# W1's products with the norm's factors ahead of the first ten adjacency chunks, and the edges' check behind them

## The chip, the cores and the metric

The kernel runs on one core of one Trainium2 chip. The metric is the time of one execution on the device, in microseconds. Three executions of the kernel before took 1035.32, 1038.75 and 1046.16 us; the median is 1038.75 us. A further execution was recorded by the hardware profiler: it took 1032.22 us, with a span of 1030.4 us between its first and last instruction. All rows of the trace quoted here are of that execution.

The engines have short names throughout: PE is the matrix engine (PEld its weight loads), DVE the vector engine, ACT the scalar engine, POOL the general engine and SP the one that issues most transfers. Each works through its own instructions in the order of the program and waits at an instruction until the semaphores that it names have come. L353 is line 353 of the kernel.

## What is computed

The layer takes 1250 tokens x of width 768 and 21250 edges (20000 drawn ones, and a loop for each token), sorted by destination. It adds to x a two-layer graph attention network and a kernelised attention, both on the normalised x, and then a mixture of 8 experts.

```python
xn = _layernorm(x)
x_norm = layer_norm(xn, norm_g, norm_b)              # the norm's factors: norm_g and norm_b
out1 = gat_conv(x_norm, src, dst, W1, a_src1, a_dst1, b1, 4, 192, N)
out2 = gat_conv(out1, src, dst, W2, a_src2, a_dst2, b2, 2, 96, N)
gnn = concatenate([x, out2], -1) @ Wu + bu
x = x + gnn + mix(xn)                                # kernelised attention, 12 heads
x = x + ffn(_layernorm(x))                           # 8 experts, 2 per token
# gat_conv: h = x @ W; e = leaky_relu(s_src[src] + s_dst[dst]) with s = (h * a).sum(-1)
#           alpha = softmax of e over the edges of one dst; out = sum alpha * h[src] + bias
```

Two parts of this matter for the change. The first is the adjacency: the kernel turns the list of edges into a dense matrix of counts, 1250 by 1250, so that the attention over edges becomes matrix products with a mask. The second is the product of W1 with the norm's factors: since x_norm is a scaled and shifted row, its product with W1 needs norm_g and norm_b multiplied into W1.

## The kernel before

The tokens are cut into ten tiles of 125. The edges are cut into 170 chunks of 125 in order of destination. A chunk holds edges of one destination tile, or of two where it lies near a border; this is true of edges that are spread evenly enough, and a check of the edges' tiles (L261 to L270) tells whether it is true of the edges given. Its result goes into the last column of the tile `bad`, which is read much later, to choose between this path and a general one.

`adjacency()` (L289) builds the counts. For each chunk c, DVE makes two one-hot tiles: `ohs` (L342) for the source, packed into 313 columns, and `ohd` (L346) for the destination. PE multiplies them into the sum `pe` of the destination tile (L353). There are five `ohs` tiles and four `ohd` tiles, used in turn, so DVE can be no more than four chunks ahead of PE. When a tile's last chunk is in, ACT copies the sum out and DVE takes the packed counts apart (L296 to L308). `adjacency()` is a generator: `adj(n)` (L366) runs n chunks, and the program calls it between other work.

The first stage of the program does the following. SP fetches the edges, W1 in three parts of 768 KB (L187) and x; ACT fetches the small arrays and W2. DVE and PE turn the edge lists so that a chunk lies along the partitions (L247 to L250), and DVE makes the packed source columns (L253 to L259). DVE then runs the check, and ten chunks follow (L371). Next DVE makes the columns of R, the products of W2 with its score vectors: four products and four sums (L394, L398). PE meanwhile multiplies W1 with norm_g and norm_b (L403): 12 products of a 128 by 2 weight, each of which the trace shows as two records. ACT copies the result into v1 (L408), and PE turns v1 by 8 small transposes, `by_channels` (L411).

Then comes a loop over the four heads. In each, PE transposes W1's two halves (L434), ACT copies them into wT (L435), PE multiplies wT with R (pw, L444) and ACT stores the result, scaled by norm_g, as W12 (L447). After each half and after every third product `beside(h)` (L419) runs two more chunks of the adjacency, and in the last heads also pieces of x's normalisation. At the end of a head, PE makes the constant columns from vv, the result of `by_channels` (pc, L453).

PE and DVE run this whole part in the order in which the program is written: it stands inside a manual schedule (L233 to L468). So DVE takes the check, ten chunks, R and the following chunks in just this order, and PE ten chunks, L403, the transposes and so on. Some tiles share buffers: `off` of the check, `pr` of R, `v1` and `wT` all use three buffers under the tag wT, one after the other in the order of the program.

After this stage come the transposes of x and the rest of the adjacency, beside the keys of the kernelised attention; the two attention layers; the update and the routing; and the experts.

Of the kernel before, what the change touches and what calls it, by code (L numbers as in the profile page):

```python
# [9 lines left out]
F32 = mybir.dt.float32  # L10
# [4 lines left out]
ALU = mybir.AluOpType  # L15
AX = mybir.AxisListType
# [3 lines left out]
D = 768  # L20
P = 125
NT = N // P
KD = D // 128
# [17 lines left out]
NCH = NEDGE // P  # L41
# [5 lines left out]
SLACK = 2  # L47
# [26 lines left out]
def kernel(  # L74
# [3 lines left out]
    nc = tc.nc  # L78
    ctx.enter_context(nc.allow_non_contiguous_dma("small vectors, laid out by partition"))

    def opened(**kw):
        p = tc.tile_pool(**kw)
        return p, p.__enter__()
# [42 lines left out]
    def stats_of(pool, src_tile, mv_col, tag):  # L126
        st = pool.tile([P, 2, 6], F32, tag="bnst", name=f"st_{tag}")
        for i in range(2):
            nc.vector.bn_stats(out=st[:, i, :], in_=src_tile[:, i * 384 : (i + 1) * 384])
        nc.vector.bn_aggr(out=mv_col, in_=st)  # L130

    def rstd_of(pool, mv, tag, t0, t1):

        ve = pool.tile([P, t1 - t0], F32, tag="lnve", name=f"ve_{tag}_{t0}")
        nc.vector.tensor_scalar(ve, mv[:, t0:t1, 1], 1e-5, None, op0=ALU.add)
        sd = pool.tile([P, t1 - t0], F32, tag="lnsd", name=f"sd_{tag}_{t0}")
        nc.scalar.activation(sd, ve, AF.Sqrt)
        rs = pool.tile([P, t1 - t0], F32, tag="lnrs", name=f"rs_{tag}_{t0}")
        nc.vector.reciprocal(rs, sd)
        return rs  # L140
# [36 lines left out]
    ps_, ps = opened(name="ps", bufs=2, space=PSUM)  # L177
# [5 lines left out]
    def weight(pool, ap, name, eng):  # L183
        w = pool.tile([128, KD, D], F32, tag="mw", name=name)
        r = ap.rearrange("(k p) n -> p k n", p=128)
        for k in range(0, KD, 2):
            eng.dma_start(out=w[:, k : k + 2, :], in_=r[:, k : k + 2, :])  # L187
        return w


    wgc_, wgc = opened(name="wgc", bufs=1)
    wg_, wg = opened(name="wg", bufs=2)
    gb = wgc.tile([128, KD, 2], F32, name="gb")
# [8 lines left out]
    w1_sb = weight(wgc, W1, "w1_sb", nc.sync)  # L202
# [32 lines left out]
    edges = {}  # L235
    iota = edc.tile([P, N], I16, name="iota")
    nc.gpsimd.iota(iota, pattern=[[1, N]], base=0, channel_multiplier=0)
    bad = edc.tile([P, NT + 1], F32, name="bad")
# [12 lines left out]
    for i in range(1, NPK):  # L251
# [5 lines left out]
            nc.vector.tensor_scalar(wgt, up, step, 1.0, op0=ALU.mult, op1=ALU.add)  # L257
        else:
            nc.vector.scalar_tensor_tensor(wgt, up, step, wgt, op0=ALU.mult, op1=ALU.add)  # L259

    mid_t = wgc.tile([P, NT, 17], F32, name="mid")  # L261
    nc.gpsimd.iota(mid_t, pattern=[[P, NT], [0, 17]], base=0, channel_multiplier=0, allow_small_or_imprecise_dtypes=True)
    mid = mid_t.rearrange("p a b -> p (a b)")
    off = wg.tile([P, 2, NCH], F32, tag="wT", name="off", bufs=3)
    nc.gpsimd.memset(off, 0.0)
    nc.vector.tensor_tensor(off[:, 0, SLACK:], edges["dst"][:, SLACK:], mid[:, : NCH - SLACK], ALU.is_lt)
    hi = wgc.tile([P, NCH], F32, tag="up1", name="hi", bufs=1)
    nc.vector.tensor_scalar(hi, edges["dst"], float(P), None, op0=ALU.subtract)
    nc.vector.tensor_tensor(off[:, 1, : NCH - SLACK], hi[:, : NCH - SLACK], mid[:, SLACK:], ALU.is_ge)
    nc.vector.tensor_reduce(bad[:, NT : NT + 1], off.rearrange("p a c -> p (a c)"), AX.X, ALU.max)  # L270

    def with_loops(rows, t):

        own = rows[:, t * P : (t + 1) * P]
        nc.vector.tensor_tensor(own, own, identb, ALU.add)
# [90 lines left out]
    def adj(n=NCH):  # L366
        for _ in range(n):
            if next(steps, 0) == 0:
                break

    adj(10)  # L371

    def normalised(g):

        t0, t1 = g * GT, (g + 1) * GT
        for t in range(t0, t1):
            stats_of(ln, acc[:, t, :D], mv1[:, t, :], f"a{t}")
            yield
        rs1 = rstd_of(ln, mv1, "a", t0, t1)
        yield  # L380
        for t in range(t0, t1):
            xn = acc[:, t, :D]
            nc.vector.tensor_scalar(
                xn, xn, mv1[:, t, 0:1], rs1[:, t - t0 : t - t0 + 1], op0=ALU.subtract, op1=ALU.mult
            )
            yield
# [4 lines left out]
    for h in range(H2):  # L391
        for i in range(2):
# [3 lines left out]
                a2[:, i, h * C2 : (h + 1) * C2].unsqueeze(1).to_broadcast([CH, 2 * H1, C2]), ALU.mult,  # L396
            )
            nc.vector.tensor_reduce(R[:, :, score_col[h][i] : score_col[h][i] + 1], pr, AX.X, ALU.add)  # L398

    pv1 = [ps.tile([2, D // 2], F32, tag="ac", name=f"pv1_{i}") for i in range(2)]  # L400
    for k in range(KD):
        for i in range(2):
            nc.tensor.matmul(  # L403
                pv1[i], gb[:, k, :], w1_sb[:, k, i * (D // 2) : (i + 1) * (D // 2)], start=(k == 0), stop=(k == KD - 1)
            )
    v1 = wg.tile([2, D], F32, tag="wT", name="v1", bufs=3)
    for i in range(2):
        nc.scalar.copy(v1[:, i * (D // 2) : (i + 1) * (D // 2)], pv1[i])  # L408
    vv = wgc.tile([CH, 2 * H1, 2], F32, name="vv")

    def by_channels():  # L411
        pv2 = ps.tile([CH, 2 * H1, 2], F32, tag="ac", name="pv2")
        for q in range(2 * H1):
            nc.tensor.transpose(pv2[:, q, :], v1[:, q * CH : (q + 1) * CH], ident[:2, :2])
        nc.scalar.copy(vv, pv2)

    early = (piece for g in range(2) for piece in normalised(g))

    def beside(h):  # L419

        for _ in range(2):
            adj(1)
            if h >= 2:
                next(early, 0)

    for h in range(H1):
        wT = []
        for j in range(2):
            wT.append(wg.tile([CH, D], F32, tag="wT", name=f"wT_{h}_{j}", bufs=3))
            q0 = (2 * h + j) * CH  # L430
            for b0, n in ((0, 4), (4, 2)):
                pt = ps.tile([128, 4, 128], F32, tag="tr", name=f"w1t_{h}_{j}_{b0}")
                for i in range(n):
                    nc.tensor.transpose(pt[:CH, i, :], w1_sb[:, b0 + i, q0 : q0 + CH], ident)  # L434
                nc.scalar.copy(  # L435
                    wT[j][:, b0 * 128 : (b0 + n) * 128].rearrange("p (a c) -> p a c", c=128), pt[:CH, :n, :]
                )
            beside(h)
        if h == 0:
            by_channels()  # L440
        for k in range(KD):
            pw = ps.tile([128, GW], F32, tag="pk", name=f"pw_{h}_{k}")
            for j in range(2):
                nc.tensor.matmul(  # L444
                    pw, wT[j][:, k * 128 : (k + 1) * 128], R[:, 2 * h + j, :], start=(j == 0), stop=(j == 1)
                )
            nc.scalar.activation(W12[:, k, h * GW : (h + 1) * GW], pw, AF.Copy, scale=gb[:, k, 0:1])  # L447
            if k in (2, 5):
                beside(h)
        for i, cb in enumerate((c1b, c0b)):  # L450
            pc = ps.tile([P, GW], F32, tag="ac", name=f"pc_{h}_{i}")
            for j in range(2):
                nc.tensor.matmul(  # L453
                    pc, vv[:, 2 * h + j, i : i + 1].to_broadcast([CH, P]), R[:, 2 * h + j, :],
                    start=(j == 0), stop=(j == 1),
                )
            nc.scalar.copy(cb[:, h * GW : (h + 1) * GW], pc)
# [86 lines left out]
    with tc.tile_pool(name="kpp", bufs=1) as kpp:  # L544
# [55 lines left out]
        for t0, n in ((0, 4), (4, 4), (8, 2)):  # L600
            pst = ps.tile([2 * H1, 4 * P], F32, tag="tr", name=f"pst_{t0}")
            for k in range(KD):
                nc.tensor.matmul(
                    pst[:, : n * P], wsc[:, k].rearrange("p h i -> p (h i)"), xnT[:, k, t0 * P : (t0 + n) * P],
                    start=(k == 0), stop=(k == KD - 1),
# [164 lines left out]
    with tc.If(flag > 0):  # L770


        with tc.tile_pool(name="gd", bufs=1) as gd, tc.tile_pool(name="ps_g", bufs=1, space=PSUM) as ps_g:
            for own, other in (("dst", "src"), ("src", "dst")):
# [6 lines left out]
                for tiles in PASSES:  # L781
# [3 lines left out]
                    c = 0  # L785
# [885 lines left out]
```

## Time and profile before

| | |
|---|---|
| median of three executions | 1038.75 us (1035.32 to 1046.16) |
| profiled execution | 1032.22 us, span 1030.4 us |
| ten chunks on PE | 11.62 to 15.99 us |
| L403 on PE, 24 records | 15.99 to 24.84 us |
| check of the edges on DVE, 4 instructions | 9.74 to 11.05 us |
| R on DVE, 8 instructions | 15.40 to 22.80 us |
| HBM read, written | 74.77 MB, 27.04 MB |

A row of a timeline gives the start in us from the beginning of the span, the duration in us, the engine, the line, the operation, the tile written and the tiles read, the sizes, and how many instructions were merged; in brackets stands how long the engine had been idle and what ended that. Consecutive instructions of one kind are merged, so the ten chunks are one row of PE. The granted clock is the share of full speed at which the matrix engine was allowed to run. Its record begins at 18.07 us, and for the time before that the tables print 1.00.

### The profile page before, as it was taken

Reading aid. Unit: us, or ns where it says so; the run is one execution under the profiler, and the core shown is the slowest. Engines: PE = TensorE matmul, PEld = TensorE weight load, DVE = VectorE, ACT = ScalarE, POOL = GpSimd, SP = SyncE. Lnnn points to the kernel's source line nnn. Section 1 sums busy time; section 2 is a strip of 40 time slices with the busy share of each in tenths; the row PEclk is TensorE's granted clock in tenths of the full one; section 3 lists DMA queues with packets and bytes.
Section 4 is the critical chain, followed back from the end, with each engine's and each line's share of the span. In section 5 each row is a group of like instructions: output and inputs, shape, how many; then the busy total and the mean of one; then the engine's idle time right before and its main releaser. Section 6 shows DMA issues by size and latency. Waiting matters only on the chain. (4 is left out here: it accounts for less than half of the span.)

```text
span 1030.4 us, 12127 instructions
## 1 busy us (share of the span) xinstructions
PE 955.1 (93%) x4323; PEld 655.1 (64%) x4323; DVE 635.3 (62%) x1407; ACT 386.2 (37%) x662; POOL 137.1 (13%) x148
## 2 busy tenths in 40 slices
PE   6899999999999999999999999999998889999970
PEld 2785455545665476777776865567678667767750
DVE  7699555304858467677768839255687554445441
ACT  0653333310000075555655800064566254323320
POOL 1001010000000000000000012110100311357633
PEclk9999999999999999999999999999998889999995
DMA  8410000032241100000023323111252357356443
GB/s 205 146 50 18 19 15 23 25 124 106 80 149 60 51 34 1 25 25 25 2 79 119 113 73 115 51 56 45 86 184 97 123 183 248 100 185 176 154 126 90
DMA packets 55169, 92.43 MB, mean 90 GB/s; under 512 B 22697, under 2 KB 29033, under 8 KB 55099
## 3 DMA queue, kind: packets, MB, share of 16 engines
q1 hardware_dynamic: 30970, 73.64, 20.7%
q0 software_dynamic: 15904, 17.02, 5.9%
q10 hardware_dynamic: 8224, 0.89, 0.7%
q8 instruction: 39, 0.64, 0.3%
q14 instruction: 32, 0.25, 0.1%
HBM read 74.77 MB, written 27.04 MB: 99 GB/s over the span
## 5 line engine op out<-in xcount | busy, mean ns | idle before, releaser
L852 PEld LDWEIGHTS pa_a<-acc,p_a 125*125 125x125 f32 x800 | 133.6, 187 | 17.1 <-issue 6.7
L852 PE MATMUL pa_a<-acc,p_a 125*125 125x197 f32 x800 | 141.6, 332 | 0.8 <-DVE h L876 0.5
L842 ACT ACTIVATE e_a<-rowt_a,s 125x625 f32<-125x625 f32 x80 | 64.8, 816 | 127.4 <-DMA rowt_a<-ab_d 93.1
L715 PE MATMUL pg<-W,xnT 128*125 128x396 f32 x240 | 81.7, 498 | 1.8 <-DVE acc L718 1.8
L922 PE MATMUL po<-wu_sb,xnT 128*125 128x384 f32 x240 | 81.7, 488 | 1.3 <-issue 1.3
L530 PE MATMUL pk_q<-xnT,wq_sb 128*128 128x375 f32 (+1 forms) x216 | 81.6, 516 | 0.7 <-DVE acc L718 0.7
L530 PE MATMUL pk_k<-xnT,wk_sb 128*128 128x375 f32 (+1 forms) x216 | 82.0, 515 | 0.0
L848 DVE SCALAR_TENSOR_TENSOR p_a<-e_a,cntT 125x625 f32<-125x625 f32 x80 | 64.0, 806 | 28.7 <-PE pa_a L852 26.9
L846 DVE SCALAR_TENSOR_TENSOR e_a<-e_a,e_a 125x625 f32<-125x625 f32 x80 | 64.2, 807 | 22.9 <-ACT e_a L842 15.8
L493 DVE CUSTOM_DVE_ANT_0 junk<-nmr,rows 125x1250 f32<-125x1250 bf16 x40 | 58.4, 1459 | 29.2 <-DMA nmr<-nm_d 16.0
L346 DVE TENSOR_SCALAR ohd<-iota,dst_f 125x125 bf16<-125x125 int16 (+1 forms) x170 | 51.4, 302 | 39.9 <-PE pe L353 39.9
L1520 PE MATMUL po<-ew,hT 128*125 (+1 forms) x192 | 67.1, 493 | 5.5 <-DVE hT L1311 5.0
L844 ACT ACTIVATE e_a<-rowt_a,s1x 125x625 f32<-125x625 f32 x80 | 64.3, 815 | 18.7 <-DVE e_a L846 18.1
L1291 PE MATMUL ph<-ew,xTe 128*125 (+1 forms) x288 | 68.9, 390 | 0.0
L715 PEld LDWEIGHTS pg<-W,xnT 128*125 128x125 f32 x240 | 44.5, 188 | 34.8 <-DVE acc L718 2.4
L922 PEld LDWEIGHTS po<-wu_sb,xnT 128*125 128x125 f32 x240 | 44.4, 189 | 31.0 <-issue 2.0
L1291 PEld LDWEIGHTS ph<-ew,xTe 128*125 128x125 f32 x288 | 55.4, 195 | 11.8
L530 PEld LDWEIGHTS pk_q<-xnT,wq_sb 128*128 128x128 f32 x216 | 39.8, 189 | 33.5 <-issue 14.3
L342 DVE TENSOR_SCALAR ohs<-iota,smod,wgt 125x313 bf16<-125x313 int16 x170 | 60.5, 356 | 0.0
L852 PE MATMUL pa_b<-h,p_b 125*125 125x97 f32 x400 | 53.4, 285 | 6.7 <-issue 2.3
L852 PEld LDWEIGHTS pa_b<-h,p_b 125*125 125x125 f32 x400 | 51.3, 201 | 11.2 <-issue 4.7
L530 PEld LDWEIGHTS pk_k<-xnT,wk_sb 128*128 128x128 f32 x216 | 38.5, 189 | 23.3 <-issue 9.7
(348 smaller groups left out, 1459.0 us busy)
## 6 DMA issues: line engine op xcount, KB each, us to landing
y_d<-y SPq DMA_DIRECT2D x23, 375.0 KB
ew<-in_w1T SPq DMA_DIRECT2D x8, 768.0 KB
ew<-in_w2T SPq DMA_DIRECT2D x8, 768.0 KB
nmr<-nm_d SPq DMA_DIRECT2D x20, 305.2 KB
rowt_a<-ab_d SPq DMA_DIRECT2D x8, 610.4 KB
x_d<-acc SPq DMA_DIRECT2D x10, 376.0 KB
acc<-in_x SPq DMA_DIRECT2D x10, 375.0 KB
xr<-in_x SPq DMA_DIRECT2D x10, 375.0 KB
```

Of the source, the lines that this page charges most:

```text
L342: nc.vector.tensor_scalar(oh_s[:, :TH], iota[:, :TH], smod[:, c : c + 1], wgt[:, c : c + 1], op0=ALU.is_equal, op1=ALU.mult)
L493: nc.vector.tensor_tensor_reduce(out=junk, in0=nm, in1=row, scale=1.0, scalar=-3.0e38, op0=ALU.add, op1=ALU.max, accum_out=mx_col)
L530: nc.tensor.matmul(pk[:, :w], w_sb[:, k, f * 128 : (f + 1) * 128], xnT[:, k, t0 * P : (t0 + n) * P], start=(k == 0), stop=(k == KD - 1),)
L715: nc.tensor.matmul(pg, xnT[:, k, t * P : (t + 1) * P], W12[:, k, cs], start=(k == 0), stop=(k == KD - 1))
L842: nc.scalar.activation(e1, rowt[:, 0, :], AF.Exp, bias=s[:, h, 0, u : u + 1])
L844: nc.scalar.activation(e2, rowt[:, 1, :], AF.Exp, bias=sx[:, h, u : u + 1])
L846: nc.vector.scalar_tensor_tensor(e1, e1, 1.0, e2, op0=ALU.min, op1=ALU.max)
L848: nc.vector.scalar_tensor_tensor(p, e1, 1.0, cntT[:, u, hf * HN : (hf + 1) * HN], op0=ALU.min, op1=ALU.mult)
L852: nc.tensor.matmul(pas[i][:, :cw], p[:, i * P : (i + 1) * P], hv, start=(u == 0), stop=(u == NT - 1))
L922: nc.tensor.matmul(po[:, hf, :384], xnT[:, k, ts], wu_sb[:, k, cs], start=(k == 0), stop=False)
L1291: nc.tensor.matmul(ph, xT[:, k, :], ew1[:, whose_r[q], k, :].rearrange("p o i -> p (o i)"), start=(k == 0), stop=(k == KD - 1),)
L1520: nc.tensor.matmul(po[:, hf, :384], hT[:, c, :], ew2[:, e_r, c, hf * 384 : (hf + 1) * 384].rearrange("p o n -> p (o n)"), start=(c == 0), ...
```

## The change

Three pieces of the program change places, and nothing is added or taken away. W1's products (L403) and the two copies into v1 (L408) stand ahead of the call of the first ten chunks. The check of the edges stands behind these ten chunks, with POOL's iota and memset for it. `by_channels` stands directly ahead of the loop over the heads, no longer inside its first turn.

```diff
-    mid_t = wgc.tile([P, NT, 17], F32, name="mid")
-    nc.gpsimd.iota(mid_t, pattern=[[P, NT], [0, 17]], base=0, channel_multiplier=0, allow_small_or_imprecise_dtypes=True)
-    mid = mid_t.rearrange("p a b -> p (a b)")
-    off = wg.tile([P, 2, NCH], F32, tag="wT", name="off", bufs=3)
-    nc.gpsimd.memset(off, 0.0)
-    nc.vector.tensor_tensor(off[:, 0, SLACK:], edges["dst"][:, SLACK:], mid[:, : NCH - SLACK], ALU.is_lt)
-    hi = wgc.tile([P, NCH], F32, tag="up1", name="hi", bufs=1)
-    nc.vector.tensor_scalar(hi, edges["dst"], float(P), None, op0=ALU.subtract)
-    nc.vector.tensor_tensor(off[:, 1, : NCH - SLACK], hi[:, : NCH - SLACK], mid[:, SLACK:], ALU.is_ge)
-    nc.vector.tensor_reduce(bad[:, NT : NT + 1], off.rearrange("p a c -> p (a c)"), AX.X, ALU.max)
...
+    pv1 = [ps.tile([2, D // 2], F32, tag="ac", name=f"pv1_{i}") for i in range(2)]
+    for k in range(KD):
+        for i in range(2):
+            nc.tensor.matmul(
+                pv1[i], gb[:, k, :], w1_sb[:, k, i * (D // 2) : (i + 1) * (D // 2)], start=(k == 0), stop=(k == KD - 1)
+            )
+    v1 = wg.tile([2, D], F32, tag="wT", name="v1", bufs=3)
+    for i in range(2):
+        nc.scalar.copy(v1[:, i * (D // 2) : (i + 1) * (D // 2)], pv1[i])
     adj(10)
+    mid_t = wgc.tile([P, NT, 17], F32, name="mid")
...
+    nc.vector.tensor_reduce(bad[:, NT : NT + 1], off.rearrange("p a c -> p (a c)"), AX.X, ALU.max)
...
+    by_channels()
     early = (piece for g in range(2) for piece in normalised(g))
...
-        if h == 0:
-            by_channels()
```

In the changed kernel W1's products are line L363, the copies into v1 L368, the first chunks' product L341, the check L373 to L381, R L404 and L408, and pw L443.

More of the change, by code (lines that the diff above doesn't have):

```diff
@@ L369, in adj @@
                 break
-    adj(10)
+    pv1 = [ps.tile([2, D // 2], F32, tag="ac", name=f"pv1_{i}") for i in range(2)]
[7 more added lines that the diff above has]
+        nc.scalar.copy(v1[:, i * (D // 2) : (i + 1) * (D // 2)], pv1[i])
+    adj(10)
+    mid_t = wgc.tile([P, NT, 17], F32, name="mid")
+    nc.gpsimd.iota(mid_t, pattern=[[P, NT], [0, 17]], base=0, channel_multiplier=0, allow_small_or_imprecise_dtypes=True)
+    mid = mid_t.rearrange("p a b -> p (a b)")
+    off = wg.tile([P, 2, NCH], F32, tag="wT", name="off", bufs=3)
+    nc.gpsimd.memset(off, 0.0)
+    nc.vector.tensor_tensor(off[:, 0, SLACK:], edges["dst"][:, SLACK:], mid[:, : NCH - SLACK], ALU.is_lt)
+    hi = wgc.tile([P, NCH], F32, tag="up1", name="hi", bufs=1)
+    nc.vector.tensor_scalar(hi, edges["dst"], float(P), None, op0=ALU.subtract)
+    nc.vector.tensor_tensor(off[:, 1, : NCH - SLACK], hi[:, : NCH - SLACK], mid[:, SLACK:], ALU.is_ge)
+    nc.vector.tensor_reduce(bad[:, NT : NT + 1], off.rearrange("p a c -> p (a c)"), AX.X, ALU.max)
     def normalised(g):
@@ L398 @@
             nc.vector.tensor_reduce(R[:, :, score_col[h][i] : score_col[h][i] + 1], pr, AX.X, ALU.add)
[L400 to L408, printed above, removed]
     vv = wgc.tile([CH, 2 * H1, 2], F32, name="vv")
```

## The prediction

> **What bounds the kernel now.** I read the page's busy shares first. TensorE is busy over nine tenths of the span, and its row of slices stands at 9 from the third slice to the thirtieth, so a delay that reaches TensorE early has hardly anywhere to be absorbed. The change lies in the first 35 us, where the shares say nothing, so I read next a table of stretches (columns: busy us and count of PE, PEld, DVE, ACT, POOL; granted clock; DMA share; GB/s).
>
> ```profile
> PE 955.1 (93%) x4323; PEld 655.1 (64%) x4323; DVE 635.3 (62%) x1407; ACT 386.2 (37%) x662; POOL 137.1 (13%) x148
> ...
> 16.00:24.80 8.80, 8.80 (x25) 2.07 (x24) 8.66 (x17) 1.75 (x2) 0.00 (x0) 1.00 0.71 186
> 24.80:36.00 11.20, 10.42 (x72) 9.17 (x71) 3.05 (x14) 6.50 (x17) 0.00 (x0) 1.00 0.69 185
> 36.00:50.00 14.00, 11.86 (x79) 10.36 (x79) 12.41 (x44) 9.02 (x21) 1.29 (x1) 1.00 0.32 126
> 50.00:100.00 50.00, 46.90 (x258) 33.66 (x258) 49.92 (x184) 23.65 (x59) 4.81 (x9) 1.00 0.11 36
> ```
>
> From 16 to 24.8 both engines are full: PE makes W1's products with the factors while DVE makes the R columns. From 24.8 to 36 PE sets the pace and DVE idles for 8.1 us, held up by the ring of one-hot tiles. From 50 to 100 DVE is full. After 100 PE is (49.91 of 50 us to 150, 513 of 520 to 670). The timeline of PE and of DVE shows the order inside this:
>
> ```profile
> 11.62 4.43 PE L353 MATMUL pe<-ohs,ohd 125*125 125x314 bf16 x10 [4.66 <-DVE ohd L346]
> 15.99 8.91 PE L403 MATMUL pv<-w_sb,gb 128*2 128x384 f32 x24
> 24.84 0.86 PE L434 MATMUL w1t<-ident,w_sb 128*96 128x128 f32 x6
> 25.53 0.43 PE L353 MATMUL pe<-ohs,ohd 125*125 125x314 bf16 x2
> ...
> 27.72 2.39 PE L444 MATMUL pw<-R,wT 96*128 96x198 f32 x12
> ```
>
> ```profile
> 9.74 0.33 DVE L266 TENSOR_TENSOR off<-dst_f,mid 125x168 f32<-125x168 f32 x1
> ...
> 11.05 0.36 DVE L342 TENSOR_SCALAR ohs<-iota,smod,wgt 125x313 bf16<-125x313 int16 x1
> ...
> 15.40 0.95 DVE L394 TENSOR_TENSOR pr<-R,a 96x768 f32<-96x768 f32 x1
> ...
> 22.80 0.35 DVE L342 TENSOR_SCALAR ohs<-iota,smod,wgt 125x313 bf16<-125x313 int16 x1
> ...
> 30.29 0.29 DVE L346 TENSOR_SCALAR ohd<-iota,dst_f 125x250 bf16<-125x250 int16 x1 [2.03 <-PE pe L353]
> 35.36 0.16 DVE L296 TENSOR_SCALAR bad<-pe 125x1 f32<-125x1 f32 x1 [4.78 <-PE pe L353]
> ```
>
> The reader is to see three things. PE idles 4.66 us before the first chunk. The ten chunks then run as fast as DVE hands out pairs of one-hots (11.05 to 15.40 is 4.35 us, 0.435 a pair). And DVE's R block, 15.40 to 22.80 (7.40 us), runs wholly under PE's L403: the two 8 us blocks cover each other.
>
> Last, when does W1 arrive? L403 needs it, so this decides how early the moved products can start. SP and ACT issues that wait for a W1 part show it:
>
> ```profile
> SPq L217 <- DMA w_sb<-in_W: 8.1, 1, 8.1
> ```
>
> This is the first tile of x, issued at 13.23 when W1's second part had landed; ACT's b1T at 9.57 follows the first part in the same way and wb's second half at 15.97 the third. The trace's landings read 9.55, 13.22 and 15.83.
>
> **The change, part by part.**
>
> *Products ahead of the chunks.* PE no longer idles to 11.62; it waits for W1's first part and starts L363 (L403 of before) at 9.6. Behind this wait stand all ten chunks, which need only DVE. The 24 records of the 12 products are of two speeds in before: the first starts lie 0.640 us apart, those after 18.07 lie 0.322 apart. The first eight records (first part of W1) at the slow pitch end at 9.6 + 5.12 = 14.7. If the clock comes up there, sixteen at 0.322 make 5.15, and the products end at E = 19.9; parts two and three have landed by the time they are needed.
>
> When does the clock come up? The row first: L403 became dense at 15.99 and got fast at 18.07, 2.1 us later, but 6.4 us after the first chunk at 11.62. [...]
>
> *Chunks behind the products.* DVE starts its one-hots 1.31 us earlier (9.74, where the check stood), but it owns four ohd and five ohs tiles and stops before the fifth ohd until PE has done chunk 0, at 19.9 + 0.3 = 20.2. So DVE stands still from about 11.6 to 20.2. Then ohd 4 and five pairs at 0.435: the last ohd starts at 22.4. In before this was done at 15.40.
>
> *Check of the edges.* Four DVE instructions, 9.74 to 11.05 = 1.31 us. They ran while PE was idle; now they stand at 22.55 to 23.9, ahead of the R block, on the path. POOL's iota and memset for them (0.42 and 0.37 us) go behind the five ohs memsets and are wanted only at 22.5: nothing.
>
> *R block.* 23.9 + 7.40 = 31.3. Its second product now waits until PE's by_channels transposes have read v1 (shared buffers of tag wT); those come about 23.3, it is due at 25.7: covered by 2 us.
>
> *What PE waits for.* After the chunks (23.0) PE does the 8 small transposes of by_channels and six of W1, to about 24.2, and then meets chunk 10, whose one-hots follow the R block on DVE: 31.3 + 0.27 + 0.25 + 0.05 = 31.8. Before, this product started at 25.53 without a wait. Behind it in PE's queue are chunk 11 (32.3), six more transposes (0.70) and two chunks (0.37), then pw at about 33.5, against 27.72. The 0.46 us that by_channels took in before's loop is out of it and is already in this number. The lag at pw is 33.5 - 27.7 = 5.75 us (in general E - 14.1). ACT's copies of the first half of wT need R's second product reduced (27.6), under this wait, so they cost nothing.
>
> *Clock.* The new idle of PE, 24.2 to 31.8, is long. What an idle of this sort does, this trace shows late in the run:
>
> ```profile
> 679.50 3.78 PE L852 MATMUL pa_b<-h,p_b 125*125 125x97 f32 x20 [2.30 <-issue]
> ...
> 676.84:680.25 3.41, 1.11 (x11) 1.05 (x11) 3.11 (x5) 3.41 (x6) 0.78 (x1) 1.00 0.01 3
> 680.25:683.67 3.42, 3.42 (x17) 3.21 (x16) 2.54 (x3) 2.59 (x5) 1.44 (x1) 0.50 0.12 24
> ```
>
> A stretch of 3.41 us with 1.11 of work was followed by 3.42 us at clock 0.50. The new idle is over twice as long, so PE resumes at half clock. By the rows it stays there 2.1 to 6.4 us after it is dense again at 32.4, half of it lost: 1.05 to 3.2 us. [...] I take 2.0, the middle of the rows, since some transposes and paced chunks stand there.
>
> *Is it given back?* Up to 36 us PE sets the pace (10.42 of 11.20 us), and DVE stops at the same two places, L346 at 30.29 and L296 at 35.36, for chunk products of PE. So DVE takes over PE's lag whole, and from there on it is itself the bound to 100, then PE. Between 36 and 110 us DVE waits only 4.6 us in all, 3.7 for PE, 0.9 for ACT. I give nothing back.
>
> *Sum.* 5.75 + 2.0 = 7.7 us. On the profiled execution, 1032.22 us with a span of 1030.4, it is 1039.9. That execution lies 6.5 us under the median of the three runs, 1038.75; on the median it is 1046.4. Bounds: 4.3 + 1.05 = 5.3 (E = 18.4) and 6.4 + 3.2 = 9.6 (E = 20.5).
>
> **The rivals.** *Only the queue wait counts* (0.18): the clock is fast soon after 9.6 and is hardly missed after the idle, because the first work there is paced by DVE anyway. 4.3 to 5.7 us, 1043.7. For it: two of the four chunks after the idle come at DVE's 0.435. Against it: the pw products, 200 ns each, follow without a pause.
>
> *The lag is refunded* (0.10), the case that is not slower. The place is 36 to 100 us, where PE idles 2.14 + 3.10 = 5.24 us and DVE 1.67. If PE's idle there is what carries the schedule, up to 6.9 us return and the result is +0.8, 1039.5. It decides when the late engine in that stretch is PE alone, with DVE's one-hots standing ready at 36. Against it: DVE is filled 49.92 of 50 us there, and its ring ties it to PE's lag.
>
> [...]
>
> That PE did not take the new order isn't to be feared: its instruction order is fixed in the program, and the built kernel has L363 ahead of the chunks.
>
> **How the numbers follow.** The forecast has 0.57. One per cent, 10.4 us, is about what a measurement can tell from no change: the three runs of before span 10.8 us. Faster by over 1% is left to scatter, 0.03. Slower by over 1% is 0.13 of the half-clock case and 0.12 of the forecast when scatter adds 3 us: 0.25. The rest, 0.72, is within 1%. The range goes from 1040, which leaves out most of the refund, to 1053, the half-clock case.
>
> **What the profile after would show.** L363 starting at 9.6 with pauses for W1 or slow records, ending near 20. DVE idle some 8 us before its fifth ohd at 20.2. R ending near 31. PE idle 7 to 8 us before chunk 10 and a granted clock of 0.50 after it. pw at 33 to 34, and the whole run behind it later by about as much. I am wrong if W1 lands far from 9.55 and 15.83, if PE meets chunk 10 without a wait, or if the lag at 36 us is not there at 100.

## The result and the profile after

In a comparison of the two kernels on one chip, 16 runs of each, the changed kernel took 1044.65 us in the median (1036.68 to 1054.86) and the kernel before 1035.03 us (1030.52 to 1046.16). The ratio of the times is 1.0077, with a 95% interval of 1.0052 to 1.0102: on 1035.03 us that is slower by 8.0 us (5.4 to 10.6). The ratio is taken over fast runs alone, without the changed kernel's two slowest (1053.55 and 1054.86 us), and so lies below the quotient of the medians, 1.0093. The forecast was 7.7 us. The profiled execution took 1044.05 us, with a span of 1042.2 us.

The page's busy shares of the changed kernel show nearly the same busy times in a longer span: PE 959.6 us for 955.1, DVE 635.6 for 635.3.

```profile
span 1042.2 us, 12127 instructions
...
PE 959.6 (92%) x4323; PEld 658.1 (63%) x4323; DVE 635.6 (61%) x1407; ACT 385.7 (37%) x662; POOL 138.1 (13%) x148
```

So the loss is waiting, and a slower clock for a while. The timeline of PE in the changed kernel shows where:

```profile
9.33 9.58 PE L363 MATMUL pv<-w_sb,gb 128*2 128x384 f32 x24 [2.36 <-DMA w_sb<-in_W]
18.84 3.22 PE L341 MATMUL pe<-ohs,ohd 125*125 125x314 bf16 x10
22.00 0.53 PE L414 MATMUL pv<-ident,v 2*96 2x2 f32 x8
22.46 1.10 PE L435 MATMUL w1t<-ident,w_sb 128*96 128x128 f32 x6
30.86 0.96 PE L341 MATMUL pe<-ohs,ohd 125*125 125x314 bf16 x2 [7.29 <-DVE ohd L334]
...
33.41 3.75 PE L443 MATMUL pw<-R,wT 96*128 96x198 f32 x12
```

PE makes W1's products from 9.33 to 18.84, then the ten chunks in 3.2 us, and after 14 small transposes (8 of `by_channels`, 6 of W1) it has nothing: chunk 10 comes at 30.86 after 7.29 us of idle PE, for a one-hot of DVE. The timeline of DVE over the same time says why DVE was so late:

```profile
19.23 0.26 DVE L334 TENSOR_SCALAR ohd<-iota,dst_f 125x125 bf16<-125x125 int16 x1 [7.26 <-PE pe L341]
...
21.58 0.33 DVE L377 TENSOR_TENSOR off<-dst_f,mid 125x168 f32<-125x168 f32 x1
...
22.89 0.94 DVE L404 TENSOR_TENSOR pr<-R,a 96x768 f32<-96x768 f32 x1
...
30.29 0.35 DVE L330 TENSOR_SCALAR ohs<-iota,smod,wgt 125x313 bf16<-125x313 int16 x1
...
42.40 0.16 DVE L284 TENSOR_SCALAR bad<-pe 125x1 f32<-125x1 f32 x1 [4.78 <-PE pe L341]
```

DVE itself stood for 7.26 us before the fifth `ohd`, whose tile was held by chunk 0, and chunk 0 stood in PE's queue behind the products. Then came the rest of the one-hots, the check (21.58 to 22.89) and R (22.89 to 30.29). First DVE waits for PE, then PE for DVE, and neither 7 us block lies beside the other's any more. The table of stretches (columns as in the prediction: busy us and count of PE, PEld, DVE, ACT, POOL; granted clock; DMA share; GB/s) shows the clock:

```profile
12.80:22.90 10.10, 9.66 (x41) 3.50 (x40) 3.60 (x16) 2.39 (x4) 0.00 (x0) 1.00 0.90 212
22.95:36.60 13.65, 6.36 (x24) 5.54 (x23) 11.22 (x26) 2.44 (x6) 0.00 (x0) 0.50 0.58 165
36.60:50.00 13.40, 12.85 (x80) 11.51 (x80) 7.82 (x29) 7.05 (x18) 1.29 (x1) 1.00 0.33 127
50.00:100.00 50.00, 45.64 (x271) 34.68 (x270) 48.32 (x173) 27.63 (x68) 3.75 (x8) 1.00 0.11 36
```

From 22.95 to 36.60 PE is granted half its clock, and of that 5.74 us lie behind chunk 10. In the kernel before no stretch of half clock follows the release at 18.07 in this part.

How the lag grows, from the two traces (after less before; at chunk 10 the 0.46 us of `by_channels` are taken off, since they stand ahead of it now):

| mark | before | after | lag |
|---|---|---|---|
| chunk 10 on PE | 25.53 | 30.86 | 4.87 |
| first pw on PE | 27.72 | 33.41 | 5.69 |
| count of the first tile on DVE (`bad<-pe`) | 35.36 | 42.40 | 7.04 |
| sum of `bad` on PE (end of the adjacency) | 209.27 | 216.56 | 7.29 |
| last start of pa_a (products of the first attention layer) | 598.46 | 605.00 | 6.54 |
| end of the span | 1030.4 | 1042.2 | 11.8 |

By 42 us everything is lost that is lost, and to 605 us little returns. The last row is that of two single executions. The stretch from the last pa_a to the end took between 428 and 447 us in the thirteen traces of this study, with no order by the kernel's first 50 us; the 8.0 us of the ratio is the better number for the whole.

### The profile page after: what moved, and what is told of

Same layout as the page of the kernel before. It is cut to its first block, busy times and chain, and to the rows that moved or that the text cites. A ratio compares the mean times of both kernels' runs of the same rounds, so it can differ in the third digit from the quotient of the medians.

```text
span 1042.2 us, 12127 instructions
## 1 busy us (share of the span) xinstructions
PE 959.6 (92%) x4323; PEld 658.1 (63%) x4323; DVE 635.6 (61%) x1407; ACT 385.7 (37%) x662; POOL 138.1 (13%) x148
## 3 DMA queue, kind: packets, MB, share of 16 engines
q1 hardware_dynamic: 30970, 73.64, 20.5%
## 5 line engine op out<-in xcount | busy, mean ns | idle before, releaser
L1519 PE MATMUL po<-ew,hT 128*125 (+1 forms) x192 | 70.1, 511 | 5.5 <-DVE hT L1310 5.0
L1290 PEld LDWEIGHTS ph<-ew,xTe 128*125 128x125 f32 x288 | 55.6, 196 | 11.9
L1519 PEld LDWEIGHTS po<-ew,hT 128*125 128x125 f32 x192 | 36.1, 196 | 29.4 <-issue 5.4
```

The lines of the kernel that those rows point to most:

```text
L1290: nc.tensor.matmul(ph, xT[:, k, :], ew1[:, whose_r[q], k, :].rearrange("p o i -> p (o i)"), start=(k == 0), stop=(k == KD - 1),)
L1519: nc.tensor.matmul(po[:, hf, :384], hT[:, c, :], ew2[:, e_r, c, hf * 384 : (hf + 1) * 384].rearrange("p o n -> p (o n)"), start=(c == 0), ...
```

## The experiments

Each kernel was compared with the kernel before on the same chip (whose medians there were 1038.7 to 1039.2 us); the row of the changed kernel is that of the first comparison, in which the kernel before had 1035.03 us. So the ratios can be set side by side, the medians of that row and of the others can't. The marks are those of the profile, in us; c10 is chunk 10 on PE, "count" the first tile's count on DVE and "sum" the sum of `bad` at the end of the adjacency.

| kernel | c10 | first pw | count | sum | median | ratio to before (95%) |
|---|---|---|---|---|---|---|
| before | 25.53 | 27.72 | 35.36 | 209.27 | | 1 |
| after | 30.86 | 33.41 | 42.40 | 216.56 | 1044.65 | 1.0077 (1.0052 to 1.0102) |
| e1_check_front | 30.48 | 33.03 | 41.28 | 215.45 | 1040.82 | 1.0036 (0.9999 to 1.0072) |
| e2_check_behind | 25.05 | 27.24 | 34.88 | 208.90 | 1036.59 | 0.9971 (0.9934 to 1.0007) |
| e3_busy_pe | 31.77 | 34.32 | 42.21 | 216.38 | 1043.08 | 1.0032 (1.0005 to 1.0060) |
| e9_busy_longer | 32.00 | 33.24 | 40.93 | 216.49 | 1042.80 | 1.0049 (1.0023 to 1.0074) |
| e4_r_in_gap | 27.92 | 30.25 | 38.83 | 213.66 | 1039.59 | 1.0000 (0.9968 to 1.0032) |
| e5_ring | 29.60 | 32.15 | 40.99 | 208.76 | 1035.49 | 0.9965 (0.9937 to 0.9992) |
| e7_after_ring10 | 23.65 | 26.20 | 34.21 | 201.04 | 1030.72 | 0.9943 (0.9918 to 0.9968) |
| e6_before_ring10 | 26.88 | 29.07 | 36.71 | 203.54 | 1030.99 | 0.9924 (0.9899 to 0.9950) |
| e11_before_ring8_7 | 26.88 | 29.07 | 36.71 | 203.30 | 1032.32 | 0.9967 (0.9934 to 1.0000) |
| e8_ring10_check_later | 22.34 | 23.89 | 31.54 | 199.70 | 1029.96 | 0.9932 (0.9905 to 0.9958) |
| e10_before_ring10_check_later | 25.05 | 27.19 | 34.83 | 201.67 | 1028.90 | 0.9915 (0.9878 to 0.9951) |

### One part alone: the check of the edges

e1 is the changed kernel with the check put back to its old place, ahead of `adj(10)` and of the one-hots, so that of the change only the products' move is left:

```diff
+    mid_t = wgc.tile([P, NT, 17], F32, name="mid")
...
+    nc.vector.tensor_reduce(bad[:, NT : NT + 1], off.rearrange("p a c -> p (a c)"), AX.X, ALU.max)
...
     adj(10)
-    mid_t = wgc.tile([P, NT, 17], F32, name="mid")
...
-    nc.vector.tensor_reduce(bad[:, NT : NT + 1], off.rearrange("p a c -> p (a c)"), AX.X, ALU.max)
```

> The changed kernel with the check of the edges back in front of the chunks; W1's products and by_channels stay ahead. Theory (the chunks wait behind the products, and R behind the chunks): DVE makes the check while it would wait anyway, so R starts 1.31 us earlier than in the changed kernel, at 21.6, chunk 10 meets PE at 29.5, pw starts at 32.1 and the first tile's count on DVE (L296 of before, 35.36) falls at 41.1: 5.7 us behind the kernel before, about 1.0055 of its time. Rival (the check behind the chunks is what costs): pw returns to 27.7, ratio 1.000.

e2 is the kernel before with the same block moved from its old place to behind `adj(10)`, so that only the check's move is made.

> The kernel before with only the check moved behind the ten chunks; W1's products stay behind the chunks. Theory: the chunks start at 10.3, not 11.6, and PE takes up the products up to 1.3 us earlier, while R starts at 15.4 as before and ends well ahead of its use: pw at 26.4 to 27.7, ratio 0.998 to 1.000. Rival (the moved check is a cost of 1.3 us by itself): pw at 29.0, ratio 1.001.

PE's timeline of e1:

```profile
9.74 10.11 PE L374 MATMUL pv<-w_sb,gb 128*2 128x384 f32 x24 [2.78 <-DMA w_sb<-in_W]
19.78 3.22 PE L352 MATMUL pe<-ohs,ohd 125*125 125x314 bf16 x10
...
30.48 0.95 PE L352 MATMUL pe<-ohs,ohd 125*125 125x314 bf16 x2 [6.22 <-DVE ohd L345]
```

and of e2:

```profile
10.44 4.44 PE L342 MATMUL pe<-ohs,ohd 125*125 125x314 bf16 x10 [3.48 <-DVE ohd L335]
14.81 9.62 PE L403 MATMUL pv<-w_sb,gb 128*2 128x384 f32 x24
24.35 0.86 PE L434 MATMUL w1t<-ident,w_sb 128*96 128x128 f32 x6
25.05 0.43 PE L342 MATMUL pe<-ohs,ohd 125*125 125x314 bf16 x2
```

From the products' end to chunk 10 it is 30.48 - 19.78 = 10.70 us in e1 and 30.86 - 18.84 = 12.02 us in the changed kernel. The difference, 1.32 us, is the check's 1.31. In e1's profile the products ended 0.94 us later, which hides most of this in the mark itself; the count is 1.1 us earlier. In e2 the chunks start 1.18 us earlier and the count comes 0.48 earlier; its ratio can't be told from 1. So the check behind the ten chunks costs its 1.3 us only together with the other move, when DVE's R is what PE waits for. The products' move is the main part: with it alone the count is 5.9 us later than before, of the 7.0. The times agree with the marks, but the two kernels' intervals overlap.

### The clock

e3 and e9 are the changed kernel with extra work on PE in the wait: 8 or 11 more of W1's products, whose result nothing reads, ahead of chunk 10. The diff is that of e3; e9 has 11 for 8 and 10 for 7.

```diff
+            if h == 0 and j == 0:
+                pd = ps.tile([2, D // 2], F32, tag="ac", name="pd")
+                for k in range(8):
+                    nc.tensor.matmul(pd, gb[:, k % KD, :], w1_sb[:, k % KD, : D // 2], start=(k == 0), stop=(k == 7))
             beside(h)
```

> The changed kernel with eight more W1 products, whose result is not used, on PE between the first transposes of W1 and chunk 10, where PE waits from 23.3 to 30.9. Theory (part of the lag is the half clock that follows this wait): chunk 10 meets PE at 30.9 as in the changed kernel, but at full clock: no granted clock of 0.50 after 31, pw at 32.9, the first tile's count at 40.1 in place of 42.4, ratio about 1.0045. Rival (the clock is no part of the lag): the count at 42.4, ratio 1.0068; or the extra products come late and add up to 1 us.

> The changed kernel with eleven more W1 products on PE in its wait, not eight; with eight PE stood still for the last 2.3 us and the clock fell to 0.50 from 31.6 to 35.0. Theory (the half clock after the wait is part of the lag): the clock stays at 1.00 from about 14.5 on, and the lag of the first tile's count is that of chunk 10's product less 0.46, where in the changed kernel it grows from 4.9 to 7.0: with the products ended by 31.3 the count falls at 40.5 or before, ratio 1.0045. Rival (something else makes the time from chunk 10 to the count longer): the growth of about 2 us stays.

In e3 the added products ended at 29.5, PE stood for 2.28 us, and the clock still fell, for 31.62 to 35.03 us. It took only a part of the slow stretch away, which is a miss of its plan: its count, 42.21, is that of the rival (42.4) and not that of the theory (40.1). Still, from chunk 10, which came 0.91 us later than in the changed kernel, to the count it took 10.44 us, 1.10 less than there. The longer chain of e9 was made to keep the clock throughout. PE's timeline of e9:

```profile
23.43 8.64 PE L442 MATMUL pd<-w_sb,gb 128*2 128x384 f32 x22
32.00 0.48 PE L341 MATMUL pe<-ohs,ohd 125*125 125x314 bf16 x2
...
33.24 2.45 PE L447 MATMUL pw<-R,wT 96*128 96x198 f32 x12
```

and e9's stretches:

```profile
22.83:26.25 3.42, 3.42 (x9) 0.84 (x8) 3.35 (x5) 0.00 (x0) 0.00 (x0) 0.50 1.04 269
26.25:36.00 9.75, 9.75 (x44) 4.99 (x43) 8.06 (x23) 2.83 (x7) 0.00 (x0) 1.00 0.48 147
```

Here PE was never idle from 22.83 to 36.00 and had its full clock from 26.25, though it too lost it for 3.42 us before. The added products ended late, so chunk 10 starts 1.14 us later than in the changed kernel. Yet the first pw comes 0.17 us earlier and the count 1.47 us earlier. From chunk 10 to the count it takes 8.93 us, for 11.54 in the changed kernel and 9.83 in the kernel before (9.37 without `by_channels`). The 12 pw products alone take 2.45 us for 3.75. So the half clock costs 11.54 - 9.37 = 2.17 us, and with the clock kept nothing of it is left. (That e9 lies even 0.44 us under 9.37 is not the clock's doing: its PE, coming late, has no wait there, while in the kernel before PE waits 0.23 us for ACT's copy into wT. Measured against e9, the cost would be 2.61 us.) Against 9.37 the cost is 1.43 in e1, 1.07 in e3 and 2.02 in e5, for 4.23, 3.26 and 5.42 us of half clock behind chunk 10: about a third of the slow time, not the half that, by an estimate from the starts of W1's products (0.640 us apart before the release at 12.71, 0.322 after it), a stretch full of dense products would lose.

By the sum of `bad` e9's gain is gone (216.49 for 216.56), and its ratio and the changed kernel's have overlapping intervals. So what the clock costs is shown at 42 us; that it is worth 2 us at the end is not.

### Why R is late: the ring of one-hots

If the four `ohd` tiles are what holds DVE, and with it the check and R, a longer ring has to bring R forward with the products left where the change puts them. The added tiles lie in the memory of MO, a tile that is filled only much later, and v1 gets memory that R doesn't need. The diff is that of e5; e7 has 10 for both 9s:

```diff
     ohs = [adp.tile([P, TH + 1], BF16, name=f"ohs_{i}", bufs=1) for i in range(5)]
+    spare_b = MO.rearrange("p a c -> p (a c)").bitcast(BF16)
+    ohs += [spare_b[:P, i * 314 : (i + 1) * 314] for i in range(5)]
+    ohds = [spare_b[:P, 1600 + i * 256 : 1600 + i * 256 + 2 * P] for i in range(9)]
...
-            oh_d = adp.tile([P, 2 * P], BF16, tag="ohd", name=f"ohd_{c}", bufs=4)
+            oh_d = ohds[c % 9]
...
-    v1 = wg.tile([2, D], F32, tag="wT", name="v1", bufs=3)
+    v1 = xnT[0:2, 0, :D]
```

> The changed kernel with ten buffers for ohs and nine for ohd instead of five and four (the added ones and v1 lie in tiles that are not in use yet). Theory (DVE stops at the fifth ohd, so R stands behind PE's products): DVE runs through ten chunks by 14.2, check by 15.5, R by 22.9; PE ends the products at 18.8, does ten chunks without a pause by 20.3 and waits for chunk 10 only to 23.4: pw at 25.0, the first tile's count at 32.7, 2.7 us ahead of the kernel before, ratio 0.9975. Rival (it is the arrival of W1 and the place of the products in PE's queue that cost, whatever the ring): pw still at 33, ratio 1.007.

> The changed kernel with ten ohs and ten ohd buffers, so that DVE can make all of the first ten chunks ahead of PE; with nine it stopped at the tenth. Theory (R stands behind PE's products by the ring alone): DVE ends the chunks at 14.3, the check at 15.6, R at 23.1; PE waits for chunk 10 only to 23.6 and pw starts at 25 to 26, the first tile's count on DVE at 32.7 to 33.5, 2 to 2.7 us ahead of the kernel before instead of 7 behind; with the later gain of 6 us the ratio is 0.992. Rival (W1's arrival and the order on PE cost, whatever the ring): the count at 41 or later, ratio 0.997 or more.

e5, with ten `ohs` and nine `ohd`, missed by one tile. DVE stopped before the tenth `ohd` as it had before the fifth, as its timeline shows:

```profile
20.15 0.26 DVE L337 TENSOR_SCALAR MO<-iota,dst_f 125x125 bf16<-125x125 int16 x1 [5.85 <-PE pe L344]
```

R stood behind it still, and PE waited 7.02 us before chunk 10. Its marks up to 41 us are the rival's; that its time is nevertheless under that of the kernel before comes from a later part, which e6 below is about. PE's timeline of e7, with ten of each:

```profile
9.32 9.95 PE L366 MATMUL pv<-w_sb,gb 128*2 128x384 f32 x24 [2.19 <-DMA w_sb<-in_W]
...
23.65 0.96 PE L344 MATMUL pe<-ohs,MO 125*125 125x314 bf16 x2 [1.64 <-DVE MO L337]
```

DVE runs through its ten pairs, the check (14.38) and R (15.68 to 23.08) without a stop, under PE's products. The wait before chunk 10 is 1.64 us instead of 7.29 and the count comes at 34.21 instead of 42.40. Of the change itself nothing is undone in e7; the ring is longer, and v1 has memory of its own. So the ring's limit is what carried the loss. The times say the same: with the ring of ten in both, the kernel before (e6 below) has a ratio of 0.9924 and the changed one 0.9943, with overlapping intervals. The count came 0.7 us later than expected; the clock was at half here too, from 23.73 to 27.14.

e4 asked the same without a longer ring: R is taken after four chunks, into the time in which DVE stood. The check goes into the first turn of the loop over the heads, and v1 out of the shared buffers as in e5.

```diff
-    adj(10)
+    adj(4)
+    score_col = ((C2, HC - 2), (2 * C2 + 1, HC - 1))
+    for h in range(H2):
+        for i in range(2):
...
+            nc.vector.tensor_reduce(R[:, :, score_col[h][i] : score_col[h][i] + 1], pr, AX.X, ALU.add)
+    adj(6)
...
+        if h == 0:
+            mid_t = wgc.tile([P, NT, 17], F32, name="mid")
```

> The changed kernel with its short ring; DVE makes R after the first four chunks, in the time in which it stands still, and the check of the edges goes into the first turn of the loop over the heads (v1 and off lie in a tile that is not in use yet). Theory (R's place behind the stalled chunks is what costs): R ends near 20, chunks 5 to 10 follow at DVE's pace to 23, chunk 10 meets PE without a long wait at 23.5 to 24.5, pw starts at 25.5 to 27, the first tile's count at 33 to 35.5, against 42.4 in the changed kernel; ratio 0.998 to 1.000. Rival (any order with the products in front costs): the count above 38.

DVE's timeline of e4:

```profile
11.43 0.26 DVE L334 TENSOR_SCALAR ohd<-iota,dst_f 125x125 bf16<-125x125 int16 x1
15.28 0.95 DVE L374 TENSOR_TENSOR pr<-R,a 96x768 f32<-96x768 f32 x1 [3.60 <-DMA a<-in_a_src]
...
22.68 0.36 DVE L330 TENSOR_SCALAR ohs<-iota,smod,wgt 125x313 bf16<-125x313 int16 x1
```

R could not start at 11.7: the score vectors landed only at 15.3, 3.60 us later. R then ended at 22.68, and PE, done with chunk 3 at 19.2, waited 4.08 us for chunk 4. The count came at 38.83, past the 38 at which the rival was to hold, and the clock was at half from 22.36 to 32.60. By the count half of the loss is won back (3.6 of 7.0 us); the time's ratio, 1.0000 (0.9968 to 1.0032), would allow more, and can't say how much. So e4 doesn't speak for the rival, since R met another wait, but it doesn't show by itself that the place of R is all that costs; e7 does that. The landing differs between runs: R began without a wait at 14.37 in e8 and at 14.52 in e10.

### The ring alone, and a version that beats both

To see what the ring is worth without the change, e6 puts the ring of e7 into the kernel before, and e11 a ring of eight `ohs` and seven `ohd`. e8 is e7 with the check in the loop's first turn; e10 is the kernel before with the ring of ten and the check there.

> The kernel before with ten ohs and ten ohd buffers, nothing moved. In the ring-of-nine run a lag of 5.6 us at 41 us was gone at 209 us, where the changed kernel still had all of its 7; so a longer ring seems to shorten the later adjacency by itself. Theory (the four-deep ring makes PE wait in every burst of seven chunks): the first 35 us as in the kernel before, then 6 us gained by 209 us, ratio 0.994. Rival (the lag was given back because a late PE finds its one-hots ready, and there is nothing to give back here): ratio 1.000.

> The kernel before with eight ohs and seven ohd buffers. The later adjacency comes in bursts of seven chunks beside the keys' products. Theory (a ring as long as a burst is enough): the sum of bad near 203 as with ten, ratio 0.993. Rival (each added buffer helps): 205 to 207, ratio 0.996.

> As the run before, and the check of the edges moved on into the first turn of the loop over the heads, where DVE waits for PE anyway. Theory: R ends at 21.8, chunk 10 meets PE without a wait at about 22.3, pw at 23.5 to 24.5, the first tile's count at 31 to 32, ratio 0.990. Rival (once R is in time, PE's own work is the bound): the same as the run before, ratio 0.992.

> The kernel before with the ring of ten and the check moved into the loop, the products in their old place behind the chunks. It is what the run with the ring of ten, the products in front and the check moved into the loop has beside the products' place. Theory (products in front are worth about 3 us once nothing of DVE stands behind them): count of the first tile at 34.9 against 31.5 there, keys' end (the sum of bad, 209.3 in the kernel before) at 203 against 199.7, ratio 0.993 to 0.994. Rival (the products' place is worth nothing): both marks as in that run.

e6 gains nothing in the first 37 us; its count is even 1.35 us later, in a profile in which the clock was released only at 20.61. But at 203.5 the sum of `bad` stands 5.7 us earlier than in the kernel before, as its theory had it (6 us) after e5 had shown such a gain unlooked for. A table of the stretch in which the keys are made (PE's busy time in the products that write one tile, granted clock, DMA share, GB/s) for the kernel before, first for the products pq_k (the features made from the keys), then for the chunks' pe, then for the keys pk_k:

```profile
76.70:209.30 132.60, 20.28 (x72) 1.00 0.08 26
76.70:209.30 132.60, 27.99 (x138) 1.00 0.08 26
76.70:209.30 132.60, 81.92 (x216) 1.00 0.08 26
```

and for e6, in the same order:

```profile
77.10:203.50 126.40, 16.31 (x72) 1.00 0.09 27
77.10:203.50 126.40, 24.20 (x140) 1.00 0.09 27
77.10:203.50 126.40, 81.55 (x216) 1.00 0.09 27
```

The same products pq_k fill 4.0 us less, the chunks' 3.8 us less, and the keys' stay. The granted clock is 1.00 in both. What differs is the order: this part is outside the manual schedule, and with the longer ring it was laid out anew. PE's timeline shows what that does to the pq_k, each of which fills one half, 64 rows, of its tile. In the kernel before:

```profile
139.58 1.05 PE L517 MATMUL pq_k<-pT_k,wb 128*64 128x500 f32 x2
...
141.70 0.58 PE L518 MATMUL pq_k<-sT_k,nh 128*64 128x500 f32 x1
141.70 0.58 PE L517 MATMUL pq_k<-pT_k,wb 128*64 128x500 f32 x1
142.12 1.00 PE L518 MATMUL pq_k<-sT_k,nh 128*64 128x500 f32 x2
```

and in e6:

```profile
138.56 1.06 PE L520 MATMUL pq_k<-pT_k,wb 128*64 128x500 f32 x4
139.45 1.01 PE L521 MATMUL pq_k<-sT_k,nh 128*64 128x500 f32 x4
```

Two products for different halves can run side by side: in e6 four take the time of two. In before this happens at 141.70, but at 139.58 and 142.12 a product has no partner ready beside it. A single record is no shorter in e6 (medians 529 ns for the one line and 478 for the other, in both kernels). In the short-ring kernels, the changed one among them, 24 of 36 possible pairs start together, in every kernel with the longer ring 32. Counted from each start to the next one on PE, the 72 products take 19.2 us before and 15.5 us in e6: the eight pairs more are 3.7 us of the gain.

The chunks' part is rather one of waits. The profile shows PE idle for one-hots for 1.8 us before and 1.5 us in e6, but a chunk's record lasts 0.30 us while a ready next one starts after 0.13, so a short wait hides under the record before it. From one chunk to the next, the steps of over 0.15 us exceed 0.134 us by 3.7 us in all before (21 steps) and by 1.6 us in e6 (6 steps). By this estimate some 2 us of the chunks' gain are shorter waits, which is what the theory of e6 had named. Order and ring were not varied apart from each other, so why the longer ring leads to this order stays open. e11's ring of eight and seven gives the same sum within 0.3 us (203.30); its time, whose interval reaches 1.0000, is not told from that of the kernel before.

The last pair tells what the products' new place is worth once the ring no longer stands in its way. PE's timeline of e8:

```profile
22.34 0.79 PE L344 MATMUL pe<-ohs,MO 125*125 125x314 bf16 x2 [0.32 <-DVE MO L337]
...
23.89 2.40 PE L434 MATMUL pw<-R,wT 96*128 96x198 f32 x12
```

Its count comes 3.3 us earlier than e10's (31.54 for 34.83), of the 4.66 us that PE stands idle ahead of the first chunk in the kernel before, and its sum of `bad` 2.0 us earlier (e8's clock was at half once more, from 44.20 to 47.61). In the times nothing of it is to be seen: 0.9932 (0.9905 to 0.9958) for e8, 0.9915 (0.9878 to 0.9951) for e10. e10, with the products in their old place, has the lowest median measured, 1028.90 us. It beats the kernel before and the changed kernel; that it beats e6, e7 or e8 can't be said.

## Why the prediction was right, step by step

**The products' start and end.** L363 started at 9.33 (forecast 9.6) and ended at 18.84 (19.9). The term was over-sized by 1.1 us because the clock came up at 12.71, 3.4 us behind the products' start, instead of at 14.7: 5.3 records at 0.640 us and 18.7 at 0.322 make 9.4 us. That it would come up at 14.7, and with it the forecast's end at 19.9, was the author's estimate; no run shows it there. In the kernels with the products in front the clock came up 3.0 us (e4) to 5.2 us (e3) behind their start, at 12.12 to 14.55 us, and the products ended between 18.4 and 19.8, so the forecast's 19.9 lies just behind the latest end seen. Its bounds, E = 18.4 and 20.5, count the 2.1 and the 6.4 us of the kernel before's row from 9.6 on; the runs fall between the two delays. With the measured end the forecast's own relation, E - 14.1, gives a lag of 4.7 us, close to the 4.87 at chunk 10.

**The ring.** DVE stopped before the fifth `ohd`, for 7.26 us (forecast about 8). With ten tiles (e7) the stop is gone and R ends at 23.08, for 22.80 in the kernel before: it is this stop that delays R.

**Check and R.** The check took 21.58 to 22.89 on the path (1.31 us, as forecast), and R 7.40 us to 30.29. Between the products' end and chunk 10 lay 12.02 us, forecast 11.9. e1 shows the check's part of it by itself.

**What PE waits for.** 7.29 us before chunk 10 (7 to 8). The lag at the first pw was 5.69 us, forecast 5.75, but that match is luck, two deviations that cancel: the queue's part was 4.87 us, for the products ended early, and 0.8 us of the clock's cost stood already ahead of pw, where the forecast had none.

**Clock.** 2.2 us, forecast 2.0, within 1.05 to 3.2. The mechanism differs in one point: the clock did not fall by the idle wait. It fell at 22.95, 0.6 us before the wait began at 23.57, behind chunks of which the last six came in DVE's steps of 0.435 us and amid the small transposes; and in e9 it fell at 22.83, where no wait followed at all. In the changed kernel it then stayed at half for 5.7 us behind chunk 10. The size, too, is met partly by luck: the stretch was near the upper end of the forecast's 2.1 to 6.4 us, and about a third of it was lost, not half.

**Given back: nothing.** Right to 209 us: the lag was 7.04 us at the first count and 7.29 at the sum of `bad`. At the last pa_a it was 6.54.

The sum of the measured parts at 42 us is 4.87 + 2.17 = 7.04 us, forecast 7.7; the ratio says 8.0. Of the rivals, "only the queue wait counts" has its size of the wait right (4.3 to 5.7) but leaves out the clock, which e9 shows at 42 us; the time of the whole alone (5.4 to 10.6 us) hardly tells the two apart. The refund didn't come: between 42 and 209 us the lag grew. The half-clock case of the chances, in which the products keep the pitch of 0.640 us to their last record and end at 25.0, fell with the release at 12.71 and with ends of 18.4 to 19.8 in every kernel that has the products first.

One reading of the kernel before was off, without a part in the sum: of the 8.1 us that DVE idles from 24.8 to 36, only 3.4 us (three waits before an `ohd`) are the ring's. The wait of 4.78 us before `bad<-pe` is for the last chunk of the first tile.

## What to carry to other kernels

Before a block is moved ahead of a piece of producer and consumer work on another engine's queue, count how many tiles the producer may run ahead, and look what stands behind those pieces in the producer's own order: here four tiles were enough to pass 7 us from PE's queue to DVE's R and back to PE. Where two engines' long blocks cover each other, a change of order on one of them uncovers both: the idle time filled in front (3.3 us at the first count, once the ring had ten tiles) is to be weighed against that. And a longer ring can change the order of a later part that a scheduler lays out, here so that more half-tile products ran side by side: look at the whole run, for the gain measured here lay 40 to 170 us behind the place where it was sought.

## What was not expected of the hardware

The granted clock fell while work still flowed. In the changed kernel it was at half from 22.95 us, and only at 23.57 came the idle time; e9's fall at 22.83 has no idle time near it. In the 3.41 us before the fall PE's records cover 2.98 us in the changed kernel and 2.97 us in e9. What stands there is thin work: six chunks in steps of 0.435 us, where a ready one starts after 0.13, then the eight small transposes of `by_channels` and the first of W1's. The stretch that the prediction shows late in the kernel before, 676.84 to 680.25 us, had 1.11 us of work when half clock followed; here it was nearly three times as much. Whether the slow pace, the transposes or something else let it fall was not separated. In the kernel before, the ten chunks of 11.62 to 15.99, all in steps of 0.435 us, did not bring the clock up: the products behind them still started up to 0.640 us apart, and it was released at 18.07, after 2.1 us of them. In e3 the fall came at 31.62, after only 2.1 us without work (PE idles from 29.49 to 31.77). The stretches of e3 show it:

```profile
27.00:31.00 4.00, 2.49 (x8) 0.51 (x6) 3.93 (x5) 0.85 (x2) 0.00 (x0) 1.00 0.54 150
31.00:35.00 4.00, 3.23 (x13) 2.83 (x14) 3.89 (x18) 0.85 (x2) 0.00 (x0) 0.58 0.32 123
```

The half-clock stretches in the first 50 us lasted whole multiples of 3.41 us: 13.65 in the changed kernel, 3.42 in e9, 3.41 in e3, 10.24 in e1 (24.47 to 34.71) and in e4. The release in the kernels with the products in front came between 12.12 and 14.55 us, and waits of 6.2 to 7.3 us (e1, e5 and the changed kernel) cost 1.4 to 2.2 us; that the cost turns on where among these steps a wait falls is the author's estimate from the two. How much work keeps the clock up was not measured.
